# Scores kept with a row to a partition: norms from ScalarE's squares, rows scaled, then transposed by block transfers and VectorE

## The chip, the cores and the metric

The kernel runs on one core of one Trainium2 chip. The metric is device time in microseconds (us) for one execution. "Before" is the median of six executions. Five engines work on it: TensorE (PE in the profile, with PEld for its weight loads), VectorE (DVE), ScalarE (ACT), GpSimd (POOL), and SyncE (SP), which issues most DMAs.

## The reference

A graph network of two layers works on `x`, 64 batches of 256 nodes with 512 features, with one adjacency matrix of 256 x 256 zeros and ones. Cut to what is computed:

```
h   = relu(layernorm(x))
q, k, v = h @ Wq.T, h @ Wk.T, h @ Wv.T
rel = adj.T * (q @ k.T)                      # per batch, 256 x 256
rel = rel / norm(rel, over the last axis)    # each row n divided by its own norm
x   = x + rel @ v                            # layer 0
h   = relu(layernorm(x))
x   = x + (adj @ h) @ weight + bias          # layer 1
```

The row norm is the matter here. It is a sum over m for every row n of `rel`, and `rel @ v` also sums over m.

## The kernel before

**Tiling.** Work goes in 32 pairs of batches (`NP` = 32, `NB` = 2 batches in each). A pair has 512 tokens, held as `TC` = 4 chunks of 128 partitions, numbered c = 2b + n. Everything is float32. Most products are done by `winograd` (L165): a product of 2 x 2 blocks in seven block products instead of eight, collected in three PSUM banks (a, c, a, c, a, b, a). After each product a `take` reads the bank. In `project_v`, `project_g` and `scores`, takes 0, 1, 2 and 6 are ScalarE copies and takes 3, 4, 5 are VectorE adds; in `mix` all seven are VectorE adds. A product that adds to a bank must wait until the take before has read it: product 3 (bank c) waits for take 1, product 4 (bank a) for take 2, product 6 (bank a) for take 4.

**Stages of a pair.** `project_v` (L323) makes v. `project_g` (L305) makes G = h Wq'Wk, so that the scores are G h'. `scores` (L336) makes the masked scores in `rel`. `attend` (L368) makes `rel @ v` and adds it to x. `ln1` (L394) is the second layer norm, `gather` (L423) multiplies by the adjacency, and `mix` (L446) by the weight; `mix` ends the pair, and GpSimd issues the store.

**Scores before.** `rel` has m on the partitions and n along the free axis. That is the form that `attend` needs as its stationary operand (L384), but the norm's sum then runs over partitions. So ScalarE squares (L358), GpSimd adds the two halves of m into `sqs` (L365), and `attend` begins with four float32 products of `sqs` by a column of ones into the bank `pn` (L374), each 128 x 128 by one column and each recorded as two passes. ScalarE takes the root (L376), VectorE the reciprocal (L377), and the result scales the rows when `attend` adds to x (L387).

**Transposing h by blocks.** The layer norm of h for a later pair is written by ScalarE, then `place_blocks` (L282) moves its 32 x 32 blocks to their transposed places with 16 DMAs of 64 KB on SP's queue, and `transpose_blocks` (L292) turns the blocks in place with eight VectorE transposes of 128 x 256 (L298). There is one buffer `blocks`, so a `place_blocks` waits until the transposes of the one before have read it.

**Order of the work.** The setup and `pairs` (L507), up to the call of `steady`, are ordered by a planner. `steady` (L529) is written out by hand for PE, DVE and ACT: each of these runs its instructions in program order, and the `side` lists say after which product a step of another stage is put on its engine. SP and GpSimd are still ordered by the planner, and an instruction of `pairs` that the planner reckons ready late is put in among those of `steady`. In the loop, iteration i runs on PE: `attend(i)`, `project_v(i+1)`, `scores(i+1)`, `gather(i)`, `project_g(i+2)`, `mix(i)`. `transpose_blocks(i+3)` is done beside `gather(i)` and `place_blocks(i+4)` after `mix(i)`. The ends differ: the first pairs are prepared in `pairs`, with `scores(0)` and `project_g(1)` before the loop, and iteration 30 (`last_but_one`) has no `project_g`: it runs `gather(30)`, then at once `attend(31)`, then `mix(30)`.

Of the kernel before, what the change touches and what calls it, by code (L numbers as in the profile page):

```python
# [9 lines left out]
F32 = mybir.dt.float32  # L10
F32R = mybir.dt.float32r
I32 = mybir.dt.int32
# [7 lines left out]
def kernel(  # L20
# [55 lines left out]
    work = ctx.enter_context(tc.tile_pool(name="work", bufs=1))  # L76
    whole = ctx.enter_context(tc.tile_pool(name="whole", bufs=2))
    small = ctx.enter_context(tc.tile_pool(name="small", bufs=3))
    ps_m = ctx.enter_context(tc.tile_pool(name="ps_m", bufs=7, space=bass.MemoryType.PSUM))
    ps_n = ctx.enter_context(tc.tile_pool(name="ps_n", bufs=1, space=bass.MemoryType.PSUM))  # L80

    X, H, HL, G, GS, V, R, H2, Y = ({} for _ in range(9))

# [125 lines left out]
    def product_of_tokens(left, right):  # L209

        def product(bank, n, start):
            for b in range(NB):
                for d in range(HC):
                    nc.tensor.matmul(  # L214
                        bank[:, ts(b, P)], left[n][:, d, ts(b, P)], right[n][:, d, ts(b, P)],
                        start=(start and b == 0 and d == 0), stop=(d == HC - 1),
                        skip_group_check=True,
                    )
        return product
# [116 lines left out]
    def scores(i):  # L336

        left, right = HL.pop(i), G.pop(i)
        rel = work.tile([P, NB, NC, N], F32, tag="rel", name=f"rel_{i}")
        sq = work.tile([P, NB, NC, N], F32, tag="sq", name=f"sq_{i}")  # L340
        sqs = work.tile([P, NB, N], F32, tag="sqs", name=f"sqs_{i}")
        R[i] = (rel, sqs)

        def take(t, k, bank, first):
            dst = rel[:, :, t, ts(k, P)]
            src = bank[:, :HT_].rearrange("p (b n) -> p b n", b=NB)
            if first:
                nc.scalar.copy(dst, src)
            else:
                nc.vector.tensor_add(dst, src, dst)  # L350

        def mask(t):
            nc.vector.tensor_mul(
                rel[:, :, t], rel[:, :, t], adj_sb[:, t : t + 1, :].to_broadcast([P, NB, N])
            )

        def square(t):
            nc.scalar.activation(sq[:, :, t], rel[:, :, t], AF.Square)  # L358

        winograd(product_of_tokens(left, right), take, {5: [lambda: mask(0)]})  # L360
        return (
            lambda: mask(1),
            lambda: square(0),
            lambda: square(1),
            lambda: nc.gpsimd.tensor_tensor(sqs, sq[:, :, 0], sq[:, :, 1], ALU.add),  # L365
        )

    def attend(i, side={}):  # L368
        (rel, sqs), v, xt = R.pop(i), flat(V.pop(i)), flat(X[i])
        pn = ps_n.tile([P, TC], F32, tag="pn", name="pn")  # L370
        for b in range(NB):
            for n in range(NC):
                c = b * NC + n
                nc.tensor.matmul(pn[:, c : c + 1], sqs[:, b, ts(n, P)], ones, start=True, stop=True)  # L374
        rn = small.tile([P, TC], F32, tag="rn", name="rn")
        nc.scalar.activation(rn, pn, AF.Sqrt)  # L376
        nc.vector.reciprocal(rn, rn)  # L377
        for b in range(NB):
            for n in range(NC):
                c = b * NC + n  # L380
                pm = ps_m.tile([P, 512], F32, tag="pm", name="pu")
                for m in range(NC):
                    nc.tensor.matmul(  # L383
                        pm[:, :D], rel[:, b, m, ts(n, P)], v[:, b * NC + m, :],  # L384
                        start=(m == 0), stop=(m == NC - 1),
                    )
                nc.vector.scalar_tensor_tensor(  # L387
                    xt[:, c, :], pm[:, :D], rn[:, c : c + 1], xt[:, c, :],
                    op0=ALU.mult, op1=ALU.add,
                )  # L390
                run(side.get(c, ()))


# [64 lines left out]
                nc.sync.dma_start(out=outs[i][:, :, t], in_=xt[:, :, t])  # L458


    low = work.tile([P, NC * N], I32, tag="sqs", name="low")
# [5 lines left out]
    pf = ps_n.tile([P, TC], F32, tag="pn", name="pf")  # L467
# [39 lines left out]
    def pairs(exact):  # L507
        for j in range(1, 5):
            load(j)
        transposes_by_matmul(0)  # L510
        ln0_at_once(1)
        place_blocks(1)
        project_v(0)
        project_g(0)
        run(GS.pop(0))
        turned, sums = transpose_blocks(1)
        run(turned + sums)
        ln0_at_once(2)
        place_blocks(2)
        run(scores(0))  # L520
        project_g(1)
        turned, sums = transpose_blocks(2)
        run(turned + sums)
        ln0_at_once(3)
        place_blocks(3)
        with tc.manual_schedule(engines={EngineType.PE, EngineType.DVE, EngineType.Activation}):
            steady(exact)

    def steady(exact):  # L529


        for i in range(NP):
            last_but_one = i + 2 == NP
            if 0 < i < NP - 4:
                load(i + 4)
            if i + 1 < NP:
                stats, root, end, relus, uppers, lowers = ln1(i, exact)
                gs = GS.pop(i + 1)
                attend(i, {c: [stats[c]] for c in range(TC)})
                project_v(i + 1, {  # L540
                    0: [root, gs[0], end, relus[0], relus[1]],
                    1: [uppers[0], uppers[1], gs[1], lowers[0]],
                    2: [relus[2], lowers[1]],
                    3: [relus[3], uppers[2], uppers[3], gs[2]],
                    4: [lowers[2]],
                    5: [lowers[3], gs[3]],
                })
                mask, square0, square1, square_sum = scores(i + 1)
            turned, sums = [], []
            if i + 3 < NP:  # L550
                turned, sums = transpose_blocks(i + 3)
            if i + 1 < NP:
                y_steps = gather(i, exact, {
                    0: [mask, square0] + turned[0:2],
                    1: [square1, square_sum] + turned[2:4],
                    2: turned[4:6],
                    3: turned[6:8],
                })
            else:
                y_steps = gather(i, exact)  # L560
            if i + 2 < NP:
                project_g(i + 2, {
                    0: y_steps[0:1],
                    1: y_steps[1:3],
                    2: y_steps[3:4] + sums[0:1],
                    3: sums[1:2],
                    4: sums[2:3],
                    5: sums[3:4],
                })
            else:  # L570
                run(y_steps)
            if i + 4 < NP:
                stats, root, end, relus = ln0(i + 4)
                mix(i, {n: [stats[n]] for n in range(TC)} | {4: [root], 5: [end] + relus})
                place_blocks(i + 4)
            elif last_but_one:
                stats, root, end, relus, uppers, lowers = ln1(i + 1, exact)
                attend(i + 1, {c: [stats[c]] for c in range(TC)})
                mix(i, {
                    0: [root, end, relus[0], relus[1]],  # L580
                    1: [uppers[0], uppers[1], lowers[0]],
                    2: [relus[2], lowers[1]],
                    3: [relus[3], uppers[2], uppers[3], lowers[2]],
                    4: [lowers[3]],
                })
            else:
                mix(i)

    first = X[0], H[0]
    with tc.If(inexact < 1) as either:  # L590
# [32 lines left out]
```

## Time and profile before

| What | Value |
| --- | --- |
| median of six runs | 1797.51 us (1795.28 to 1798.89) |
| the profiled execution | 1797.57 us, span 1795.8 us |
| PE busy | 1765.1 us, 98% of the span |
| DVE busy | 1201.1 us, 67% |
| ACT busy | 571.1 us, 32% |
| POOL busy | 241.7 us, 13% |
| granted PE clock, mean | 0.995 |
| DMA packets under 512 B | 263120 of 290246 |
| one pair in the loop | 54.26 us from one `attend` to the next (852.84 to 907.10) |

In a line of the chain of waits the columns are start, duration, engine, tile and source line. A line of the timeline gives start, duration, engine, source line, operation, output and inputs with shapes, the number of instructions joined, and in brackets the idle time before it with what ended it. A line of windows gives, for a stretch, its length, the busy time and count of PE, PEld, DVE, ACT and POOL, and then the granted PE clock (1.00 is full), the DMA engines' busy share and GB/s.

### The profile page before, as it was taken

The page shows a single profiled execution, that of the slowest core. Times are in us where ns is not written, and L with a number is a line of the kernel's source. Part 1 is how long each engine was busy: PE and PEld are TensorE (multiplying, and loading weights), DVE is VectorE, ACT ScalarE, POOL GpSimd, SP SyncE. Part 2 cuts the span into 40 slices and gives each one's busy share as a digit, 9 for nine tenths or more (in the row PEclk, how much of TensorE's full clock was granted, in tenths as well). Part 3 has the DMA queues.
Part 4 walks back from the last instruction along what each step waited for, and adds up shares of the span by engine and source line. Part 5 has one row for each costly group of instructions (what it writes and reads, how often), then busy time and mean ns, then how long its engine had stood idle before and what let it go on. Part 6 is the DMA issues. An engine that isn't in the chain of part 4 may idle for free.

```text
span 1795.8 us, 22994 instructions
## 1 busy us (share of the span) xinstructions
PE 1765.1 (98%) x9030; PEld 1480.0 (82%) x9030; DVE 1201.1 (67%) x2216; ACT 571.1 (32%) x1071; POOL 241.7 (13%) x200
## 2 busy tenths in 40 slices
PE   7899999999999999999999999999999999999998
PEld 4778888888888888889888889888888888888886
DVE  5477666767666766766676766676767676666555
ACT  3233222333223333323332323332323332233321
POOL 0011111111101111101111101111111111011111
PEclk9999999999999999999999999999999999999999
DMA  6313321233311332311223211333212232111001
GB/s 222 47 24 71 70 45 46 52 71 71 71 40 35 68 71 71 71 36 36 71 71 70 55 47 41 71 71 71 48 50 45 71 71 71 42 45 32 24 24 49
DMA packets 290246, 105.93 MB, mean 59 GB/s; under 512 B 263120, under 2 KB 263120, under 8 KB 290128
## 3 DMA queue, kind: packets, MB, share of 16 engines
q1 hardware_dynamic: 279904, 68.19, 18.6%
q0 software_dynamic: 8592, 33.03, 5.0%
q10 hardware_dynamic: 1632, 3.15, 0.5%
q8 instruction: 72, 1.18, 0.3%
q14 instruction: 46, 0.38, 0.1%
HBM read 38.27 MB, written 33.55 MB: 40 GB/s over the span
## 4 chain that ended last, share of the span: by engine, by line
PE 93%; issue 4%; DVE 1%; DMA 0%; ACT 0%; POOL 0%; POOLq 0%; DVEq 0%
PE bank_a L202 24%; PE pu L383 12%; PE bank_a L190 12%; PE bank_c L202 12%; PE py L435 7%; PE bank_a L214 6%; PE bank_c L190 6%; PE bank_b L202 6%; PE bank_c L214 3%; PE bank_b L190 3%; PE bank_b L214 1%; PE pn L374 1%; DMA adj_sb<-in_adj_dram 0%; DVE h L416 0%; ACT h2c L245 0%
## 5 line engine op out<-in xcount | busy, mean ns | idle before, releaser
L383 PE MATMUL pu<-v,rel 128*128 128x512 f32 x512 | 227.5, 597 | 0.0
L408 POOL TENSOR_TENSOR x_ring<-x_ring,bias_bc 128x512 f32<-128x512 f32 x128 | 174.9, 1385 | 371.1 <-ACT h2c L245 371.1
L233 DVE BATCH_NORM_STATS2 st<-x_ring 128x6 f32<-128x512 f32 x256 | 175.8, 688 | 11.9 <-DMA x_ring<-in_x_dram 7.5
L383 PEld LDWEIGHTS pu<-v,rel 128*128 128x128 f32 x512 | 94.9, 190 | 107.2 <-issue 106.7
L416 DVE TENSOR_TENSOR h<-h2c,h 128x512 fp32r<-128x512 f32 x128 | 122.6, 976 | 63.1 <-ACT h L412 63.1
L451 DVE TENSOR_TENSOR x_ring<-bank_a,x_ring 128x512 f32<-128x512 f32 x128 | 88.5, 691 | 109.4 <-PE bank_a L202 105.6
L330 ACT COPY v<-bank_a 128x512 f32<-128x512 f32 x96 | 56.0, 584 | 321.0 <-PE bank_a L202 321.0
L313 ACT COPY g<-bank_a 128x512 f32<-128x512 f32 x96 | 56.2, 585 | 274.6 <-PE bank_a L190 274.6
L435 PE MATMUL py<-adjt_r,h 128*128 128x256 f32 x1024 | 130.6, 285 | 0.0
L435 PEld LDWEIGHTS py<-adjt_r,h 128*128 128x128 f32 x1024 | 124.8, 192 | 0.1
L455 POOL DMA_DIRECT2D out_dram<-x_ring x31 | 23.9, 770 | 747.9 <-issue 574.8
L202 PE MATMUL bank_a<-w_t,ys 128*128 128x256 f32 x512 | 121.1, 379 | 0.0
L202 PE MATMUL bank_a<-wv_t,hs 128*128 128x256 f32 x512 | 121.0, 379 | 0.0
L190 PE MATMUL bank_a<-hs,m_t 128*128 128x256 f32 x512 | 120.9, 379 | 0.0
L202 PEld LDWEIGHTS bank_a<-w_t,ys 128*128 128x128 f32 x512 | 97.1, 190 | 13.7 <-DVE x_ring L451 0.6
L202 PEld LDWEIGHTS bank_a<-wv_t,hs 128*128 128x128 f32 x512 | 97.3, 190 | 13.2
L190 PEld LDWEIGHTS bank_a<-hs,m_t 128*128 128x128 f32 x512 | 97.3, 190 | 13.2
L245 ACT ACTIVATE h2c<-x_ring,nb,rs 128x512 f32<-128x512 f32 x128 | 97.3, 806 | 30.0 <-DVE h L416 15.8
L245 ACT ACTIVATE h<-x_ring,nb,rs 128x512 f32<-128x512 f32 x124 | 90.8, 802 | 50.0 <-DVE nb L242 49.6
L387 DVE SCALAR_TENSOR_TENSOR x_ring<-pu,rn,x_ring 128x512 f32<-128x512 f32 x128 | 96.1, 751 | 11.6 <-PE pu L383 5.6
L238 ACT ACTIVATE rs<-rs 128x4 f32<-128x4 f32 x64 | 13.2, 207 | 266.2 <-DVE rs L237 266.2
L365 POOL TENSOR_TENSOR sqs<-sq 128x512 f32<-128x512 f32 x32 | 40.8, 1274 | 413.3 <-DVE ht L298 220.4
(124 smaller groups left out, 3263.0 us busy)
## 6 DMA issues: line engine op xcount, KB each, us to landing
x_ring<-in_x_dram SPq DMA_DIRECT2D x32, 1024.0 KB, 5.8
blocks<-h SPq DMA_DIRECT2D x496, 64.0 KB, 2.3
out_dram<-x_ring POOLq DMA_DIRECT2D x31, 1024.0 KB, 4.8
wk_sb<-in_L_gnn_Wk_dram ACTq DMA_DIRECT2D x4, 256.0 KB, 5.3
wq_sb<-in_L_gnn_Wq_dram SPq DMA_DIRECT2D x4, 256.0 KB, 6.4
wv_sb<-in_L_gnn_Wv_dram ACTq DMA_DIRECT2D x1, 1024.0 KB, 11.9
w_sb<-in_L_gnn_weight_dram ACTq DMA_DIRECT2D x1, 1024.0 KB, 16.0
out_dram<-x_ring SPq DMA_DIRECT2D x2, 512.0 KB, 4.2
```

The lines of the kernel that those rows point to most:

```text
L190: nc.tensor.matmul(bank[:, e * HT_ : (e + 1) * HT_], right[n][:, d, ts(e, P)], left[n][:, d, :], start=(start and e == 0 and d == 0), stop ...
L202: nc.tensor.matmul(bank[:, b * HD : (b + 1) * HD], left[n][:, d, ts(b, P)], right[n][:, d, :], start=(start and b == 0 and d == 0), stop=( ...
L214: nc.tensor.matmul(bank[:, ts(b, P)], left[n][:, d, ts(b, P)], right[n][:, d, ts(b, P)], start=(start and b == 0 and d == 0), stop=(d == H ...
L233: nc.vector.bn_stats(st[:, c, :], src[:, c, :])
L245: nc.scalar.activation(dst, src[:, c, :], AF.Relu, bias=nb[:, c : c + 1], scale=rs[:, c : c + 1])
L313: nc.scalar.copy(dst, src)
L383: nc.tensor.matmul(pm[:, :D], rel[:, b, m, ts(n, P)], v[:, b * NC + m, :], start=(m == 0), stop=(m == NC - 1),)
L387: nc.vector.scalar_tensor_tensor(xt[:, c, :], pm[:, :D], rn[:, c : c + 1], xt[:, c, :], op0=ALU.mult, op1=ALU.add,)
L408: nc.gpsimd.tensor_tensor(xt[:, c, :], xt[:, c, :], bias_bc, ALU.add)
L416: nc.vector.tensor_sub(dst[:, 1, c, :], whole_h[c], dst[:, 0, c, :].bitcast(F32))
L435: nc.tensor.matmul(pm[:, d, :], left[:, b * NC + m, ts(d0 + d, P)], right, start=(n == 0), stop=(n == len(terms) - 1),)
L451: nc.vector.tensor_add(dst, bank.rearrange("p (b e) -> p b e", b=NB), dst)
```

## The change

The two operands of the scores' products are exchanged, so that `rel` has n on the partitions: a row to a partition. The mask is now the transposed adjacency, and both halves of it are applied after the last product. The norm becomes four ScalarE squares of 128 x 256 that also sum along the row (`accum_out`), a root, a reciprocal, and four ScalarE copies that scale each row in place. Then `place` moves the 32 x 32 blocks with 16 DMAs of 32 KB on SP's queue into `placed`, and four VectorE transposes (`turn`) write `turned`, which `attend` uses. The squares by GpSimd's add, the products with ones, and the PSUM bank `pn` are gone (`ps_m` has 8 banks instead of 7), and `attend`'s last step is a plain add. In the loop, the scales and `place` come after take 0 of `project_g`, and the four turns after take 5 of `mix`.

```diff
-    ps_m = ... bufs=7
-    ps_n = ... bufs=1
+    ps_m = ... bufs=8
...
-                        bank[:, ts(b, P)], left[n][:, d, ts(b, P)], right[n][:, d, ts(b, P)],
+                        bank[:, ts(b, P)], right[n][:, d, ts(b, P)], left[n][:, d, ts(b, P)],
...
         def take(t, k, bank, first):
-            dst = rel[:, :, t, ts(k, P)]
+            dst = rel[:, :, k, ts(t, P)]
...
+        def square_sum(b, k):
+            nc.scalar.activation(square, rel[:, b, k], AF.Square, accum_out=rn[:, b, k : k + 1])
+        def root():
+            nc.scalar.activation(rn, rn, AF.Sqrt)
+        def inverse():
+            nc.vector.reciprocal(rn, rn)
+        def scale(b, k):
+            nc.scalar.activation(rel[:, b, k], rel[:, b, k], AF.Copy, scale=rn[:, b, k : k + 1])
+        def place():
+            rv = rel.rearrange("p b k (t m) -> p (b k t) m", m=P)
+            pv = placed.rearrange("p b k t n -> p (b k t) n")
+            for j in range(P // S):
+                for k in range(P // S):
+                    nc.sync.dma_start(out=pv[ts(j, S), :, ts(k, S)], in_=rv[ts(k, S), :, ts(j, S)])
+        def turn(b, k):
+            nc.vector.transpose(turned[:, b, :, k], placed[:, b, k])
+        def each(f):
+            return [(lambda b=b, k=k: f(b, k)) for k in range(NC) for b in range(NB)]
-        winograd(product_of_tokens(left, right), take, {5: [lambda: mask(0)]})
+        winograd(product_of_tokens(left, right), take)
...
     def attend(i, side={}):
-        pn = ps_n.tile([P, TC], F32, tag="pn", name="pn")
-        for b, n: nc.tensor.matmul(pn[:, c : c + 1], sqs[:, b, ts(n, P)], ones, start=True, stop=True)
-        nc.scalar.activation(rn, pn, AF.Sqrt)
-        nc.vector.reciprocal(rn, rn)
...
-                        pm[:, :D], rel[:, b, m, ts(n, P)], v[:, b * NC + m, :],
+                        pm[:, :D], rel[:, b, m, n], v[:, b * NC + m, :],
...
-                nc.vector.scalar_tensor_tensor(xt[:, c, :], pm[:, :D], rn[:, c : c + 1], xt[:, c, :], ...)
+                nc.vector.tensor_add(xt[:, c, :], pm[:, :D], xt[:, c, :])
...
-        run(scores(0))
+        scores_at_once(0)
...
                 y_steps = gather(i, exact, {
-                    0: [mask, square0] + turned[0:2],
-                    1: [square1, square_sum] + turned[2:4],
-                    2: turned[4:6],
-                    3: turned[6:8],
+                    0: masks + turned[0:1],
+                    1: squares[0:2] + turned[1:3],
+                    2: squares[2:4] + turned[3:5],
+                    3: [norm_root, inverse] + turned[5:8],
                 })
...
                 project_g(i + 2, {
-                    0: y_steps[0:1],
+                    0: scales + [place] + y_steps[0:1],
...
             else:
+                if last_but_one:
+                    run(scales + [place])
                 run(y_steps)
...
-                mix(i, {n: [stats[n]] for n in range(TC)} | {4: [root], 5: [end] + relus})
+                mix(i, {n: [stats[n]] for n in range(TC)} | {4: [root], 5: [end] + turns + relus})
...
             elif last_but_one:
+                run(turns)
                 attend(i + 1, {c: [stats[c]] for c in range(TC)})
...
             else:
-                mix(i)
+                mix(i, {5: turns} if i + 1 < NP else {})
```

More of the change, by code (lines that the diff above doesn't have):

```diff
@@ L78 @@
     small = ctx.enter_context(tc.tile_pool(name="small", bufs=3))
-    ps_m = ctx.enter_context(tc.tile_pool(name="ps_m", bufs=7, space=bass.MemoryType.PSUM))
-    ps_n = ctx.enter_context(tc.tile_pool(name="ps_n", bufs=1, space=bass.MemoryType.PSUM))
+    ps_m = ctx.enter_context(tc.tile_pool(name="ps_m", bufs=8, space=bass.MemoryType.PSUM))
     X, H, HL, G, GS, V, R, H2, Y = ({} for _ in range(9))
@@ L339, in scores @@
         rel = work.tile([P, NB, NC, N], F32, tag="rel", name=f"rel_{i}")
-        sq = work.tile([P, NB, NC, N], F32, tag="sq", name=f"sq_{i}")
-        sqs = work.tile([P, NB, N], F32, tag="sqs", name=f"sqs_{i}")
-        R[i] = (rel, sqs)
+        placed = work.tile([P, NB, NC, NC, P], F32, tag="placed", name=f"placed_{i}")
+        turned = work.tile([P, NB, NC, NC, P], F32, tag="turned", name=f"turned_{i}")
+        square = work.tile([P, N], F32, tag="square", name=f"square_{i}")
+        rn = small.tile([P, NB, NC], F32, tag="rn", name="rn")
+        R[i] = turned
         def take(t, k, bank, first):
-            dst = rel[:, :, t, ts(k, P)]
-            src = bank[:, :HT_].rearrange("p (b n) -> p b n", b=NB)
+            dst = rel[:, :, k, ts(t, P)]
+            src = bank[:, :HT_].rearrange("p (b m) -> p b m", b=NB)
             if first:
@@ L350, in take, with mask @@
                 nc.vector.tensor_add(dst, src, dst)
-        def mask(t):
+        def mask(k):
             nc.vector.tensor_mul(
-                rel[:, :, t], rel[:, :, t], adj_sb[:, t : t + 1, :].to_broadcast([P, NB, N])
+                rel[:, :, k], rel[:, :, k], adjt_sb[:, k : k + 1, :].to_broadcast([P, NB, N])
             )
-        def square(t):
-            nc.scalar.activation(sq[:, :, t], rel[:, :, t], AF.Square)
-        winograd(product_of_tokens(left, right), take, {5: [lambda: mask(0)]})
+        def square_sum(b, k):
+            nc.scalar.activation(square, rel[:, b, k], AF.Square, accum_out=rn[:, b, k : k + 1])
@@ L361, in scores @@
+        def turn(b, k):
[3 more added lines that the diff above has]
+        winograd(product_of_tokens(left, right), take)
         return (
[L362 to L365, printed above, removed]
-        )
+            [lambda: mask(0), lambda: mask(1)], each(square_sum), root, inverse, each(scale), place,
+            each(turn),
+        )
@@ L368, in attend, with scores_at_once @@
+    def scores_at_once(i):
+        masks, squares, root, inverse, scales, place, turns = scores(i)
+        run(masks + squares + [root, inverse] + scales + [place] + turns)
     def attend(i, side={}):
-        (rel, sqs), v, xt = R.pop(i), flat(V.pop(i)), flat(X[i])
-        pn = ps_n.tile([P, TC], F32, tag="pn", name="pn")
[L371 to L374, printed above, removed]
@@ L375, in attend @@
-        rn = small.tile([P, TC], F32, tag="rn", name="rn")
-        nc.scalar.activation(rn, pn, AF.Sqrt)
-        nc.vector.reciprocal(rn, rn)
+        rel, v, xt = R.pop(i), flat(V.pop(i)), flat(X[i])
         for b in range(NB):
@@ L383, in attend @@
                     nc.tensor.matmul(
-                        pm[:, :D], rel[:, b, m, ts(n, P)], v[:, b * NC + m, :],
+                        pm[:, :D], rel[:, b, m, n], v[:, b * NC + m, :],
                         start=(m == 0), stop=(m == NC - 1),
                     )
[L387 to L390, printed above, removed]
+                nc.vector.tensor_add(xt[:, c, :], pm[:, :D], xt[:, c, :])
                 run(side.get(c, ()))
@@ L458, in mix @@
                 nc.sync.dma_start(out=outs[i][:, :, t], in_=xt[:, :, t])
-    low = work.tile([P, NC * N], I32, tag="sqs", name="low")
+    low = work.tile([P, NC * N], I32, tag="h", name="low")
     nc.vector.tensor_single_scalar(
@@ L466 @@
     nc.vector.tensor_reduce(low_max, low, axis=mybir.AxisListType.X, op=ALU.max)
-    pf = ps_n.tile([P, TC], F32, tag="pn", name="pf")
+    pf = ps_m.tile([P, 512], F32, tag="pm", name="pf")
     nc.tensor.matmul(pf[0:1, 0:1], low_max, ones, start=True, stop=True)
@@ L547, in steady @@
                 })
-                mask, square0, square1, square_sum = scores(i + 1)
+                masks, squares, norm_root, inverse, scales, place, turns = scores(i + 1)
             turned, sums = [], []
```

## The prediction, made before the changed kernel was run

> **What bounds the kernel now.** I read the page first: which engine is full, and what the chain that ended last is made of.
>
> ```profile
> PE 1765.1 (98%) x9030; PEld 1480.0 (82%) x9030; DVE 1201.1 (67%) x2216; ACT 571.1 (32%) x1071; POOL 241.7 (13%) x200
> PE 93%; issue 4%; DVE 1%; DMA 0%; ACT 0%; POOL 0%; POOLq 0%; DVEq 0%
> blocks<-h SPq DMA_DIRECT2D x496, 64.0 KB, 2.3
> ```
>
> TensorE is the bound; work on other engines costs time only where TensorE comes to wait for it. The third line (DMA issues) prices a block transfer: 64 KB, 2.3 us to landing. Next, the chain in order of time at one pair's border:
>
> ```profile
> 904.59 1.73 PE bank_a L202 x8
> 906.32 0.79 PE pn L374 x8
> 907.10 6.97 PE pu L383 x16
> ```
>
> The norm's products hold TensorE for 0.79 us between `mix` and `rel @ v`. Third, the timeline there, for who would be late if they went:
>
> ```profile
> 904.63 0.69 DVE L451 TENSOR_TENSOR x_ring<-bank_b,x_ring 128x512 f32<-128x512 f32 x1 [0.96 <-PE bank_b L202]
> 905.43 0.16 DVE L242 SCALAR_TENSOR_TENSOR nb<-mv,rs 128x4 f32<-128x4 f32 x1
> 905.94 1.08 PEld L374 LDWEIGHTS pn<-ones,sqs 128*128 128x128 f32 x8
> 908.59 12.26 SPq L288 DMA_DIRECT2D blocks<-h  x16
> ```
>
> The four turns come after the second line, and the first load of `attend` can start where the third does. Last, both ends, where pairs don't overlap:
>
> ```profile
> 72.26 2.73 DVE L298 STREAM_TRANSPOSE ht<-blocks 128x256 f32<-128x256 f32 x8 [0.20 <-issue]
> 103.41 2.71 DVE L298 STREAM_TRANSPOSE ht<-blocks 128x256 f32<-128x256 f32 x8
> 107.35 3.78 PE L202 MATMUL bank_a<-wv_t,ht 128*128 128x256 f32 x8 [3.06 <-DVE v L332]
> 1746.34 4.07 PE L435 MATMUL py<-adjt_r,h 128*128 128x256 f32 x32
> 1752.07 7.11 PE L383 MATMUL pu<-v,rel 128*128 128x512 f32 x16
> ```
>
> and the granted clock after TensorE's wait of 3.06 us:
>
> ```profile
> 107.35:110.00 2.65, 2.65 (x6) 2.19 (x7) 2.65 (x5) 0.00 (x0) 0.00 (x0) 0.50 0.74 96
> 113.60:116.00 2.40, 2.40 (x24) 2.40 (x23) 0.01 (x1) 0.74 (x2) 0.00 (x0) 1.00 0.77 105
> ```
>
> After that wait the clock stays at half to about 113.5, over 6.2 us of work. A longer wait thus costs another 3.1 us.
>
> **In the loop: the gain.** Thirty pairs (1 to 30) have the 0.79 us in the open; those of pairs 0 and 31 lie in waits at the ends. The add in `attend` becomes plain: 751 ns (L387) to 691 (L451, also bank to x). The last one heads the chain of statistics and relus that makes TensorE wait 0.15 us in `project_v` (12.24 us for seven products of 1.727), so 0.06 comes off.
>
> **In the loop: the turns.** Each is an L298: 408 ns, starting 0.34 apart. The first group of `attend` needs the first turn only, the second group the third. That holds if waits follow the slices and not the whole tile, and they do: at 878.35 ScalarE writes a slice of `rel` while the first mask (877.91 to 878.60) works on slices interleaved with it. VectorE is free at 905.59. The transposes at 72.26 came 0.20 us behind a short reciprocal, so: start 905.79, end 906.20, load 906.25, 0.31 after 905.94. Loads run about 0.13 ahead (a load 0.27 late in `project_v` cost 0.14), leaving 0.18 us; without that gap, none. I take 0.18. The turns put the last take of `mix` at 907.2, before the first bank of `attend` is full (908.7): no cost.
>
> **In the loop: ScalarE.** Both masks now wait for take 6 (ends 878.72) and end by 880.1 instead of 879.44. A 128x512 square is 639 ns; a copy falls from 584 to 372 with half the columns, so a 128x256 square is 0.43, or 0.33 behind another. What the row sum adds no row shows: nothing to 0.2. Four squares between the copies of `gather` end it at 883.2 to 884.0, about where take 0 starts (883.91). The scales follow at 884.4: 0.33 plus 0.09 for an operand read per partition (a relu with two is 806 against 612 for a cast) is 0.42 each, to 886.1. Take 1 then ends at 886.7; product 3 loads at 886.95. No cost, with 0.4 us to spare.
>
> VectorE waits for the root, to 884.3 at worst, then ends three transposes (885.4), `y_steps` and one sum (4.2 us together before, the first at 1350 ns beside GpSimd's add that is now gone) by 889.0; take 3 came at 889.16. No cost. GpSimd's 1274 ns go at no gain.
>
> `place` starts at 886.1 on SP, idle since 867.6 and next needed at 908.6. Sixteen issues: 64 KB ones are 0.68 (10.86/16, first set) to 0.77 (12.26/16) apart, a large load holds SP 0.50; I take 0.62. With 2.1 to 2.3 to landing that is 9.3 + 2.1 = 11.4 us: landed at 897.5, eight before the turns. The cover is `project_g` and most of `mix`. Per pair: -0.79 - 0.06 + 0.18 = -0.67 us; times 30, **-20.1** (bounds: -25.5 with no wait for a turn, -16 with 0.32).
>
> **The end.** Iteration 30 has no `project_g`, so nothing covers squares, scales, place and turns. From the copies (1747.57 on), as above: squares, root and reciprocal end at 1751.7, scales at 1753.4, or 1753.8 with half of the possible row sum cost. Plus 11.4 and a turn with its signals (0.5): `attend(31)` starts at 1765.7 against 1752.07, 13.6 later, and the half clock adds 3.1: **+16.7** (14.5 to 20).
>
> **The start.** Before, the planner put the transposes of block set 1 behind the norm of pair 0 (72.26, though the set's DMAs were over by 60), and those of set 2 at 103.41, into `project_v(1)`, though the DMAs were idle from 88. So it reckons some 25 us for sixteen block transfers. New: masks end 68.3, inverse 69.7, transposes of set 1, `project_g(1)` from 70.3 to 85.5 at half clock first (before: to 86.66). Scales end 71.4, place lands 82.9, turns after take 5 at 84.4: `attend(0)` waits little. But set 2 is now queued on SP behind `place` and its transposes move, by the planner's reckoning of 13 us more, to the end of `scores(1)`, about 110. The interruption at 103 to 113 (3.06 of idle and 3.1 of clock) is gone, but set 3 may be placed only then: 112.8 + 11.5 + 2.3 = 126.6. Its transposes stand by hand in `gather(0)`, ahead of the inverse: scales to 130.4, take 1 to 131.1, while product 3 of `project_g(2)` was ready at 119.9. TensorE waits 11 us and loses 3.1; that stage ends at 141.1 against 134.5: **+6.6**. Bounds: -1.2 if set 2 keeps its place; +8.7 if SP takes set 2 before `place`, and `attend(0)` waits 13 us.
>
> **Sum.** The profiled execution took 1797.57 us (span 1795.8), the median 1797.51, so no shift: 1797.57 - 20.1 + 6.6 + 16.7 = 1800.8.
>
> **Two rules.** The Trainium skill, DMA: Bandwidth & Descriptors (Rules for kernel authors), speaks against `place`: below 64 KB a transfer is mostly overhead; Anatomy of one DMA gives 2.0 us fixed for each (on GpSimd's path). Sixteen in a row would be 33 us by it (estimate), and the sum about 1822. The trace's sixteen start 0.77 apart, so the fixed parts overlap. TensorE: Matmul & The Clock Gate (Part 1) gives a warm-up of about 3.4 us, not the 6.2 seen; by it each long wait costs 1.7 (estimate), and the sum is 1798.
>
> **Rivals.**
> - *ScalarE becomes the bound inside the pair* (slower). Take 1 queues behind four scales, and product 3 waits. It decides once scales start more than 0.52 us apart; at 0.62 it is 0.4 us in 30 pairs: +12, 1813 (1807 to 1822). For it: no row has this form. Against: the relu rows. 0.20.
> - *The ends cost less* (faster). The start stays hidden (-1.2), SP issues 32 KB at 0.50 apart (+14.5), the turns cost nothing in the loop (-25.5): 1785; halfway to the forecast, 1793. For it: smaller transfers, the planner's order unseen. 0.20.
> - *It doesn't do what it says*: waits go by whole tiles, so TensorE waits for all four turns, 1.0 us more per pair: 1831. Against: 878.35. Or the functions no longer share a table: a load is 1283 ns, but before had two in all with the same functions. 0.05.
>
> **Numbers.** The forecast has 0.55, its own range 1794 to 1807: the ends take back what the loop gains. About 0.2% (3.6 us) is what a measurement can tell from no change. Of the 0.55, 0.28 lies within it, 0.25 above, 0.02 below; the rivals add 0.20 and 0.05 above, and 0.18 below and 0.02 within. Faster 0.20, same 0.30, slower 0.50. The range 1789 to 1813 leaves out some 2 in 10.
>
> **What would show it.** Right: one pair 53.6 us; no line L374; a gap ahead of `pu` of 0.2; 15 us of idle TensorE after the last `gather` but one, and about 11 in the first `project_g` of the loop, each followed by half clock. Wrong: scales over 0.5 us apart and TensorE released by ScalarE in each `project_g`; the turns later than take 5; block set 3 landed before 119.

## The result: 0.3% slower, and the profile after

The changed kernel takes 1802.72 us (median of 16 runs, 1801.09 to 1804.35) against 1797.52 us for the one before (36 runs). The ratio is 1.0029 with an interval of 1.0022 to 1.0035. The profiled execution took 1803.25 us with a span of 1801.4 us, 5.6 us more than the span before.

First the page of the changed kernel: busy time by engine, the chain by engine, and the two block transfers among the DMA issues (count, size, median us to landing).

```profile
PE 1745.2 (97%) x8774; PEld 1448.6 (80%) x8774; DVE 1212.3 (67%) x2344; ACT 644.8 (36%) x1391; POOL 200.8 (11%) x168
PE 94%; SPq 1%; DMA 1%; ACT 1%; DVE 1%; issue 0%; ACTq 0%; DVEq 0%
blocks<-h SPq DMA_DIRECT2D x496, 64.0 KB, 2.3
placed<-rel SPq DMA_DIRECT2D x512, 32.0 KB, 2.0
```

TensorE has 19.9 us less to do in a span that is 5.6 us longer. SP's queue has appeared in the chain and the DMA's share of it has gone from 0% to 1%: TensorE now waits somewhere for a transfer. The chain of the changed kernel at a border of two pairs (start, duration, what) shows the gain and the first loss:

```profile
902.11 1.73 PE bank_b L201 x8
903.84 1.74 PE bank_a L201 x8
905.58 0.07 issue
905.65 7.11 PE pu L400 x16
```

The 0.79 us of `pn` are gone, but `pu` holds 7.11 us instead of 6.97, with 0.07 ahead of it. The timeline there says why:

```profile
903.88 0.69 DVE L465 TENSOR_TENSOR x_ring<-bank_b,x_ring 128x512 f32<-128x512 f32 x1 [0.96 <-PE bank_b L201]
904.69 0.16 DVE L241 SCALAR_TENSOR_TENSOR nb<-mv,rs 128x4 f32<-128x4 f32 x1
905.06 1.43 DVE L378 STREAM_TRANSPOSE turned<-placed 128x256 f32<-128x256 f32 x4 [0.21 <-issue]
905.62 0.30 PEld L400 LDWEIGHTS pu<-v,turned 128*128 128x128 f32 x2 [0.46 <-PE bank_a L201]
```

The first turn starts 0.21 us after the last step of the layer norm, and the first load of `attend` stands 0.11 us behind that turn's end (905.06 and at most 0.45 for one turn), not behind all four (906.49). The bracket names `bank_a`, but the time follows the turn: the first product (905.65) starts 0.59 after the first turn, and it does so too at both ends, in the lines below, where the bracket names the turn.

The two ends, by the timeline of the changed kernel. At the start:

```profile
74.36 3.20 SPq L375 DMA_DIRECT2D placed<-rel  x5
77.68 10.69 SPq L287 DMA_DIRECT2D blocks<-h  x16
88.41 7.16 SPq L375 DMA_DIRECT2D placed<-rel  x11
95.68 11.05 SPq L287 DMA_DIRECT2D blocks<-h  x16
90.09 2.73 DVE L297 STREAM_TRANSPOSE ht<-blocks 128x256 f32<-128x256 f32 x8 [2.96 <-DMA blocks<-h]
97.70 9.25 PE L400 MATMUL pu<-v,turned 128*128 128x512 f32 x16 [9.56 <-DVE turned L378]
```

SP takes five issues of pair 0's `place`, then all sixteen of block set 2, then the other eleven, and then block set 3 (from 95.68); `attend(0)` waits 9.56 us for `place`. At the end, in iteration 30:

```profile
1743.47 10.40 SPq L375 DMA_DIRECT2D placed<-rel  x16
1755.25 1.49 DVE L378 STREAM_TRANSPOSE turned<-placed 128x256 f32<-128x256 f32 x4 [10.79 <-DMA placed<-rel]
1755.84 9.62 PE L400 MATMUL pu<-v,turned 128*128 128x512 f32 x16 [16.00 <-DVE turned L378]
```

Sixteen issues 0.65 apart and the landing of the last of them stand in the open, and `attend` takes 9.62 and 9.25 us where a pair of the loop takes 7.1. The windows of the changed kernel show the granted clock, which stands behind the busy times and counts of the five engines, at 0.50 after both waits:

```profile
97.70:102.00 4.30, 4.30 (x5) 1.80 (x6) 1.34 (x4) 0.00 (x0) 0.00 (x0) 0.50 0.69 103
102.00:107.00 5.00, 5.00 (x13) 2.28 (x12) 4.20 (x10) 0.00 (x0) 0.00 (x0) 1.00 0.63 91
1755.80:1760.00 4.20, 4.16 (x5) 1.86 (x6) 1.30 (x4) 0.00 (x0) 0.00 (x0) 0.50 0.03 6
```

The ledger of the two profiled executions, from where `attend` and the stages start in the two chains:

| Stretch | before | after | difference |
| --- | --- | --- | --- |
| start to the end of `project_g(2)` | 134.48 | 141.38 | +6.9 |
| from there to `attend(30)` | 1586.62 | 1569.26 | -17.4 |
| `attend(30)` to `attend(31)` | 31.11 | 45.20 | +14.1 |
| `attend(31)` to the end of the span | 43.6 | 45.56 | +2.0 |

Together +5.6 us. In the loop a pair takes 53.70 us instead of 54.27.

### The profile page after: what moved, and what is told of

The parts are those of the page before. It is cut to its first block, busy times and chain, and to the rows that moved or that the text cites. A ratio compares the mean times of both kernels' runs of the same rounds, so it can differ in the third digit from the quotient of the medians.

```text
span 1801.4 us, 23762 instructions
## 1 busy us (share of the span) xinstructions
PE 1745.2 (97%) x8774; PEld 1448.6 (80%) x8774; DVE 1212.3 (67%) x2344; ACT 644.8 (36%) x1391; POOL 200.8 (11%) x168
## 4 chain that ended last, share of the span: by engine, by line
PE 94%; SPq 1%; DMA 1%; ACT 1%; DVE 1%; issue 0%; ACTq 0%; DVEq 0%
PE bank_a L201 24%; PE pu L400 13%; PE bank_c L201 12%; PE bank_a L189 12%; PE py L449 7%; PE bank_a L213 6%; PE bank_b L201 6%; PE bank_c L189 6%; PE bank_c L213 3%; PE bank_b L189 3%; PE bank_b L213 2%; DMA w_sb<-in_L_gnn_weight_dram 1%; SPq L375 1%; SPq L287 1%; DMA wk_sb<-in_L_gnn_Wk_dram 0%
## 5 line engine op out<-in xcount | busy, mean ns | idle before, releaser
L400 PE MATMUL pu<-v,turned 128*128 128x512 f32 x512 | 231.9, 606 | 28.4 <-DVE turned L378 26.0
L400 PEld LDWEIGHTS pu<-v,turned 128*128 128x128 f32 x512 | 96.5, 193 | 149.5 <-issue 136.2
L404 DVE TENSOR_TENSOR x_ring<-pu,x_ring 128x512 f32<-128x512 f32 x128 | 88.5, 691 | 32.8 <-PE pu L400 25.2
L297 DVE STREAM_TRANSPOSE ht<-blocks 128x256 f32<-128x256 f32 x248 | 86.9, 408 | 3.2 <-DMA blocks<-h 3.0
```

The costliest lines, as they stand in the source:

```text
L297: nc.vector.transpose(ht[:, d, half].rearrange("p (b n) -> p b n", b=NB), by_half[:, :, half, d])
L400: nc.tensor.matmul(pm[:, :D], rel[:, b, m, n], v[:, b * NC + m, :], start=(m == 0), stop=(m == NC - 1),)
L404: nc.vector.tensor_add(xt[:, c, :], pm[:, :D], xt[:, c, :])
```

## The experiments

Theory: the loop gains what the products held, less a wait for the first turn; the start and the end each lose a wait for `place`, the start's because of the order of issues on SP, the end's because nothing covers it, and each brings the half clock. The rivals: ScalarE's scales or VectorE cost time inside the pair; transfers or landing, not order and issue, bound the two ends. Times below are medians, ratios are to the kernel before.

**Pair 31 turned by TensorE** (`e1_end_by_tensore`). Eight TensorE transposes and two copies take the place of `place` and the turns, for that pair alone.

```diff
+        def by_tensore(b):
+            pt = ps_m.tile([P, 512], F32, tag="pm", name="pr")
+            for t, k: nc.tensor.transpose(pt[:, ts(t * NC + k, P)], rel[:, b, k, ts(t, P)], ident)
+            (nc.vector.tensor_copy if b else nc.scalar.copy)(turned[:, b], pt)
...
-                    run(scales + [place])
+                    run(scales + by_tensore of both batches)
...
-                run(turns)
```

> The changed kernel, with one part undone: for pair 31 alone the scaled rows are transposed by eight TensorE transposes into two PSUM banks and copied back (one copy on ScalarE, one on VectorE), instead of 16 block transfers and four turns. Theory (the end costs 16.1 us, because nothing covers the transfers): the start of the last rel @ v falls from 1755.8 to about 1746, since the wait is then squares, scales, transposes and copies (some 6 us after the last gather product); half clock may still follow, as the wait stays over 3 us. About 1792.5 us, the loop's pairs unchanged at 53.70. Rival (the loss is spread over the loop, and the end only shows it): the time falls by less than 4 us, 1799 or more.

Measured: 1789.67 us, 0.9955 (0.9941 to 0.9968), 13.0 us below the changed kernel. `attend(30)` to `attend(31)` falls from 45.20 to 33.66 us, where the kernel before has 31.11: all but 2.6 of the 14.1 us by which this stretch had grown are `place` with its turns. In all it is some 3 us more than I expected, and more than twice the 5.2 us by which the changed kernel is slower. The timeline of this run:

```profile
1741.70 0.33 PE L384 MATMUL pr<-ident,rel 128*128 128x128 f32 x1 [2.46 <-ACT rel L368]
1743.72 8.65 PE L412 MATMUL pu<-v,turned 128*128 128x512 f32 x16 [0.24 <-ACT turned L389]
```

The half clock still follows, behind a wait of 2.46 us: `attend(31)` takes 8.65.

**Pair 0 turned by TensorE** (`e2_start_by_tensore`).

```diff
-        run(masks + squares + [root, inverse] + scales + [place] + turns)
+        run(masks + squares + [root, inverse] + scales + by_tensore of both batches)
```

> The changed kernel, with one part undone: for pair 0 alone the scaled rows are transposed by TensorE as in the other run, so that nothing of pair 0 stands on the DMA queue between block sets 1 and 2. Theory (the start costs 4.6 us beside the setup, as attend(0) waits 9.6 us for turns whose transfers were split by block set 2): that wait goes, set 2's transposes may fall into project_v(1) again as before, which cost 6.2 us there; together about 1798 us. Rival (the 6.9 us are the setup's, a matter of chance): no change, 1802 to 1803.

Measured: 1796.43 us, 0.9992 (0.9983 to 1.0001), 6.3 us below the changed kernel. The timeline of this run at the start:

```profile
76.11 40.62 SPq L287 DMA_DIRECT2D blocks<-h  x32
86.69 7.03 PE L412 MATMUL pu<-v,turned 128*128 128x512 f32 x16
107.20 3.51 PE L201 MATMUL bank_a<-wv_t,ht 128*128 128x256 f32 x8 [3.09 <-DVE v L331]
```

Block sets 2 and 3 go out on SP with nothing of `place` among them, `attend(0)` starts at 86.69 without a wait, and the old interruption of `project_v(1)` is back. So the start swaps a wait of 9.6 us for one of 3.1.

**The turns after take 4 of `mix` instead of take 5** (`e3_turns_after_take4`).

```diff
-                mix(i, {...} | {4: [root], 5: [end] + turns + relus})
+                mix(i, {...} | {4: [root] + turns, 5: [end] + relus})
...
-                mix(i, {5: turns} if i + 1 < NP else {})
+                mix(i, {4: turns} if i + 1 < NP else {})
```

> The changed kernel, with one size of its schedule changed: the four turns stand after take 4 of mix (behind the small step ahead of the root) instead of after take 5. Theory (in each of 28 pairs the first load of rel @ v waits 0.28 us for the first turn, the transfers having landed some 6 us before): the wait goes, a pair takes 53.4 instead of 53.70, and the time falls by 7.8 us to about 1795. Rival (the turns only move the delay, to take 5 and the end of the relus, and TensorE waits elsewhere in mix or for the transfers): 1802 or more.

Measured: 1793.55 us, 0.9979 (0.9970 to 0.9989), 9.2 us below the changed kernel. The timeline of this run at a border:

```profile
895.88 1.42 DVE L378 STREAM_TRANSPOSE turned<-placed 128x256 f32<-128x256 f32 x4
897.99 0.16 DVE L241 SCALAR_TENSOR_TENSOR nb<-mv,rs 128x4 f32<-128x4 f32 x1
898.25 0.41 PEld L400 LDWEIGHTS pu<-v,turned 128*128 128x128 f32 x2
```

The turns are done one product earlier, the first load has no wait in brackets, and the pair takes 53.37 us instead of 53.70. The wait for the first turn cost 0.33 us in each of 28 pairs (in the last two of the loop no norm step stands ahead of the turns, and they take 53.60 and 53.37 already in the changed kernel).

**The kernel before, with the norm's products made twice** (`e4_before_norm_twice`).

```diff
-        for b in range(NB):
+        for b in range(2 * NB):
+            b = b % NB
             for n in range(NC):
...
                 nc.tensor.matmul(pn[:, c : c + 1], sqs[:, b, ts(n, P)], ones, start=True, stop=True)
```

> The kernel before, with the products of the norm by the column of ones issued twice (the second time over the same results). Theory (each set holds TensorE for 0.79 us with nothing beside it): 30 pairs by 0.79 and about 1 us at each end, 1797.5 + 25 = 1822.5 us, a pair 55.05. Rival (they run partly in the shadow of something else, so that taking them away could only have gained the 0.57 us a pair that was seen): 17 us, about 1815.

Measured: 1826.45 us, 1.0161 (1.0148 to 1.0175); the pair goes from 54.27 to 55.17, +0.90 for the second set. I had expected the 0.79 of the chain's line.

**The kernel before without the norm's products** (`e11_before_without_norm`).

```diff
-                nc.tensor.matmul(pn[:, c : c + 1], sqs[:, b, ts(n, P)], ones, start=True, stop=True)
...
-        nc.scalar.activation(rn, pn, AF.Sqrt)
-        nc.vector.reciprocal(rn, rn)
+        nc.vector.memset(rn, 1.0)
```

> The kernel before without the norm's products, root and reciprocal (the rows are multiplied by 1, so the result lacks the norm). It gives the most that the removal can bring in the loop. Theory: the 0.79 us of the products lie wholly in the open, the pair goes from 54.27 to 53.48, the ends keep their times, and thirty pairs make 1797.5 - 23.7 = 1773.8. The rival, that part of it is taken back as soon as the products go (the first load of attend waits for the last takes, or the statistics are late): pair 53.6 to 54.0 and 1778 to 1790.

Measured: 1764.40 us, 0.9818 (0.9804 to 0.9831), below both theories. Its chain at a border:

```profile
888.11 1.73 PE bank_a L202 x8
889.84 6.87 PE pu L381 x16
```

Without `pn` the piece of `pu` is 6.87 us long, where it is 6.97 behind `pn`. So the products are worth 0.79 + 0.10 = 0.89, and the pair falls from 54.27 to 53.37, -0.90. Thirty pairs make 27 us; the other 6 of the 33 (4.7 of the 31.7 between the two profiled spans) lie at the ends (`attend(0)` starts 2.7 us earlier, at 84.36), where I had put the products, with TensorE's wait for their operand, at nothing. This kernel keeps the dearer add (0.75 us, L385) and reaches the same 53.37 as the one with early turns and the plain add: the plain add is worth nothing in the loop.

**Two more ScalarE copies behind the scales** (`e10_two_more_copies`).

```diff
-                    0: scales + [place] + y_steps[0:1],
+                    0: scales + [place] + (two copies of rel[:, b, 0] into square) + y_steps[0:1],
```

> In the loop ScalarE makes two more copies of 128 x 256, of no use, right behind place, so that take 1 of project_g comes some 0.75 to 0.84 us later (0.33 to 0.42 each). In the profile of the changed kernel take 1 ends at 885.81 and product 3 starts at 886.41, with its first load some 0.13 ahead, so ScalarE has 0.46 to spare. Theory (the cover is that thin and no thinner): TensorE waits about 0.3 to 0.4 us in each of 30 project_g, the pair goes from 53.70 to 54.0 to 54.1, the time to 1812 to 1815. If the scales cost something already: the pair grows by the whole 0.75 to 0.84, and the time is 1825 or more. If the cover is much wider than it looks: 1802.7.

Measured: 1811.29 us, 1.0079 (1.0066 to 1.0093); the pair takes 54.00 us, +0.30. In its timeline:

```profile
887.66 0.83 ACT L387 COPY square<-rel 128x256 f32<-128x256 f32 x2
888.40 0.58 ACT L312 COPY g<-bank_c 128x512 f32<-128x512 f32 x1
889.03 1.59 PEld L189 LDWEIGHTS bank_c<-hs,m_sb 128*128 128x128 f32 x8 [0.44 <-ACT g L312]
```

Product 3's first load now waits for ScalarE's take 1, as the rival of the prediction had it. The added work of 0.74 us (887.66 to 888.40) cost 0.30, so 0.44 us were to spare.

**Rows scaled in the add, no scales** (`e8_rows_scaled_in_add`).

```diff
-        run(masks + squares + [root, inverse] + scales + [place] + turns)
+        run(masks + [place] + squares + [root, inverse] + turns)
...
-                    0: masks + turned[0:1],
+                    0: masks + [place] + turned[0:1],
...
-                    0: scales + [place] + y_steps[0:1],
+                    0: y_steps[0:1],
...
-                    run(scales + [place])
+                    pass
...
-                nc.vector.tensor_add(xt[:, c, :], pm[:, :D], xt[:, c, :])
+                nc.vector.scalar_tensor_tensor(xt[:, c, :], pm[:, :D], rn[:, b, n : n + 1], xt[:, c, :], ...)
```

> The changed kernel without ScalarE's scales: rows go unscaled through place, which is issued right after the masks, and attend's add multiplies by the reciprocal as before the change. Theory: in the loop the scales cost nothing now, so the pair keeps its 53.70 and gains back only the 0.06 us of the dearer last add (53.76); at the end place(31) starts some 6.6 us earlier (after the masks instead of after the scales), at the start place(0) goes out before block set 2 and attend(0) waits little, but set 2 then interrupts project_v(1): 1802.7 - 6.6 - 6 + 1.8 = 1792. The rival, that the scales cost time in the loop: the pair falls below 53.6 and the time below 1788.

Measured: 1792.82 us, 0.9976 (0.9966 to 0.9985), 9.9 us below the changed kernel. The pair keeps its 53.70: the scales cost nothing there, and neither does the dearer add. All of the gain is at the ends (`attend(30)` to `attend(31)` 39.55). The time is as I expected, but at the start not for the reason I gave, as the timeline of SP in this run shows:

```profile
67.87 3.86 SPq L375 DMA_DIRECT2D placed<-rel  x6
73.44 10.71 SPq L287 DMA_DIRECT2D blocks<-h  x16
84.19 6.52 SPq L375 DMA_DIRECT2D placed<-rel  x10
```

`place` starts 6.5 us earlier than in the changed kernel (2.1 of it because this profile's setup was faster, see the last section), and still only six of its issues go ahead of block set 2. SP even sits idle from 71.73 to 73.44, with ten issues ready behind set 2: it goes by a fixed order and does not take what is ready. `attend(0)` still waits 7.17 us.

**Pair 0's `place` from GpSimd's queue** (`e6_place0_on_gpsimd`).

```diff
+            queue = nc.gpsimd if i == 0 else nc.sync
...
-                    nc.sync.dma_start(out=pv[...], in_=rv[...])
+                    queue.dma_start(out=pv[...], in_=rv[...])
```

> Only the place of pair 0 is issued from GpSimd's queue instead of SP's. Theory: the wait of 9.56 us before attend(0) is the order on SP, where the sixteen issues of block set 2 (10.7 us) stand between the fifth and the sixth of place. Then place(0) lands by about 87, attend(0) starts at 88 to 90 with at most 1 to 3 us of wait, and the time falls by 6 to 9 us, to 1794 to 1797, unless set 2 and its transposes then hold up project_v(1). The rival, that both sets share the DMA engines and would be as late in two queues: attend(0) still at 96 to 98 and 1802.7.

Measured: 1795.98 us, 0.9990 (0.9981 to 0.9999), 6.7 us below the changed kernel. Its timeline:

```profile
73.88 9.23 POOL L376 DMA_DIRECT2D placed<-rel  x16 [70.61 <-ACT rel L368]
85.96 1.41 DVE L379 STREAM_TRANSPOSE turned<-placed 128x256 f32<-128x256 f32 x4
86.87 7.03 PE L401 MATMUL pu<-v,turned 128*128 128x512 f32 x16
107.36 3.68 PE L201 MATMUL bank_a<-wv_t,ht 128*128 128x256 f32 x8 [3.08 <-DVE v L331]
```

The same sixteen transfers, now beside those of set 2 instead of among them, are in place by 85.96, and `attend(0)` waits for nothing, while the old interruption of `project_v(1)` is back. That settles the start's wait for `place`: it is the order on SP, not the transfers.

**Half of pair 31's `place` on ScalarE's queue** (`e7_end_place_two_queues`).

```diff
-                    nc.sync.dma_start(out=pv[...], in_=rv[...])
+                    (nc.scalar if i + 1 == NP and k % 2 else nc.sync).dma_start(out=pv[...], in_=rv[...])
```

> The sixteen issues of pair 31's place are halved between SP's queue and ScalarE's. If the issue (0.65 apart on one queue, 10.4 us for sixteen) bounds it and not the transfer, eight take 5.2 us, turns start some 5 us earlier and the time is 1797.5 to 1798. If the transfers bound it (the DMA engines, the landing), nothing changes: 1802.7. Only that pair's transfers are moved, so nothing else in the trace should differ.

Measured: 1796.17 us, 0.9993 (0.9984 to 1.0002), 6.5 us below the changed kernel. Its timeline at the end:

```profile
1742.10 5.17 SPq L375 DMA_DIRECT2D placed<-rel  x8
1742.11 5.51 ACTq L375 DMA_DIRECT2D placed<-rel  x8
1748.95 1.43 DVE L378 STREAM_TRANSPOSE turned<-placed 128x256 f32<-128x256 f32 x4 [5.86 <-DMA placed<-rel]
```

Two queues issue side by side at about the pace of one each (0.65 and 0.69 apart); `attend(30)` to `attend(31)` falls by 4.93 us to 40.27. So the issue on one queue, not the transfers, bounds how soon the last block lands. The profiled span fell by 7.1 us; its other parts are 0.8 in `attend(31)` (8.77 us, see the last section) and 1.4 at the start, which this edit does not touch.

**TensorE kept busy ahead of `attend(31)`** (`e5_end_kept_busy`).

```diff
+                for _ in range(17):
+                    nc.tensor.matmul(pw_, ident, w_sb[:, 0], start=True, stop=True)
                 run(turns)
```

> Seventeen products of 128 x 512 with no use for the result (some 14.8 us at 0.87 each) fill TensorE's wait of 16.0 us before attend(31). If the clock's drop in that wait is what makes attend(31) 9.62 us instead of 6.97, it is 6.97 again, TensorE waits about 1 us for the turns, and the whole is 2.65 us shorter: 1800.1. The rival, that attend(31) is slow because its later turns or its banks come late: it stays at 9.6 and the time at 1802.7.

Measured: 1800.47 us, 1.0015 (1.0006 to 1.0024), 2.25 us below the changed kernel. In its timeline the products without use (seventeen, each recorded as two passes) fill the wait, and in its windows the clock after it is 1.00:

```profile
1739.20 14.75 PE L596 MATMUL warm<-w_sb,ident 128*128 128x512 f32 x34
1755.35 7.10 PE L400 MATMUL pu<-v,turned 128*128 128x512 f32 x16 [1.40 <-DVE turned L378]
```
```profile
1755.30:1762.50 7.20, 7.15 (x17) 3.34 (x18) 5.66 (x13) 0.00 (x0) 0.00 (x0) 1.00 0.00 1
```

From `attend(31)` to the end it is 43.05 us instead of 45.56: the half clock costs 2.5 us, as a thing of its own beside the wait.

**The three edits together** (`e9_all_three`: pairs 0 and 31 by TensorE, turns after take 4).

> The three edits on one kernel: pairs 0 and 31 turned by TensorE transposes and ScalarE/VectorE copies instead of block transfers, the four turns of the other pairs after take 4 of mix. If the three costs (start, end, wait for the first turn) lie on separate stretches of the path, their gains add up: 1802.7 - 13.0 - 6.3 - 9.2 = 1774.2, some 1.3% faster than the kernel before. The rival, that they share a wait (a start that is late anyway catches up in the loop, or TensorE is held by something else once the turns are early): between 1780 and 1790.

Measured: 1776.29 us, 0.9881 (0.9866 to 0.9896). The pair is 53.37. The gains add up but for 2.1 us of 28.5; what became of those was not settled (four executions, which lie between 1774.36 and 1776.77).

**The same, with the rows scaled in the add** (`e12_all_and_scaled_in_add`: `place` or the TensorE transposes right behind the masks, no scales).

> The kernel with all three edits, and without ScalarE's scales: unscaled rows are placed or transposed right behind the masks, and attend's add multiplies by the reciprocal. Theory: the loop has no cost from either side of the scales, so the pair stays at 53.37; at the two ends TensorE's transposes no longer wait for squares, root and scales (they waited 4.3 us at the start and 2.5 at the end), of which the start gives back part, since project_g(1) then waits for the transposes of block set 1: 1776.3 - 2 - 2 = 1772. The rival, that both ends are held by other work by now: 1776. If the dearer add (0.75 us instead of 0.69) does cost time in the loop: pair 53.43 and 1774.

Measured: 1769.78 us, 0.9851 (0.9835 to 0.9868), the fastest here with a norm in it: 1.5% below the kernel before, 1.8% below the changed one. Its timeline at the end:

```profile
1722.17 1.04 PE L384 MATMUL pr<-ident,rel 128*128 128x128 f32 x8
1723.89 0.57 ACT L389 COPY turned<-pr 128x512 f32<-128x512 f32 x1
1724.51 7.13 PE L412 MATMUL pu<-v,turned 128*128 128x512 f32 x16 [1.30 <-ACT turned L389]
```

A wait of 16.0 us has become 1.30, and the granted clock is 1.00 throughout `attend(31)`.

## Why the prediction was right, and where its steps were off

The forecast was 1800.8 us in 1789 to 1813; 1802.72 was measured. The ends do take back what the loop gains. The signs that the prediction named came in the loop and at the end (53.70 a pair, no line of the norm's products, a gap ahead of `pu`, 16.0 us of idle TensorE and then half clock), but not at the start. By steps:

**The loop: -17.4 instead of -20.1.** Three of its terms were mis-sized, and partly cancel. The products were worth 0.90 a pair, not 0.79: their line in the chain leaves out the 0.10 by which they held up the first load of `pu`. The plain add, put at -0.06, was worth nothing (53.37 with either add, and 53.70 with either); the 0.15 us of idle in `project_v` were not shortened by it, since its last piece is 1.86 to 1.87 us in all these chains. The wait for the first turn, put at 0.18, was 0.33, at the bound that I gave without the slack that loads seemed to have, and in 28 pairs instead of 30. So -0.90 + 0.33 = -0.57 a pair instead of -0.67. That waits follow slices, not the whole tile, was right.

**ScalarE and VectorE: right.** In the timeline of the changed kernel the row sum has an instruction of its own:

```profile
879.99 0.42 ACT L359 ACTIVATE square<-rel 128x256 f32<-128x256 f32 x1
880.31 0.19 ACT L359 ACTIVATION_READ_ACCUMULATOR square<-rel 128x1 f32 x1
883.64 1.70 ACT L368 ACTIVATE rel<-rel,rn 128x256 f32<-128x256 f32 x4
885.25 0.56 ACT L312 COPY g<-bank_c 128x512 f32<-128x512 f32 x1
```

0.19 us each, at the upper end of "nothing to 0.2"; the scales are 0.42 apart as worked out. Take 1 ends at 885.81 ahead of product 3 at 886.41, and the 0.44 us to spare that the two copies found are the predicted 0.4. The rival in which ScalarE becomes the bound had the right place and, by the two copies, about the right price (what is added less 0.4); its condition (scales over 0.52 apart) was not met.

**`place` in the loop: right.** It issues from 885.37 for 10.40 us, 0.65 apart against the 0.62 that I took, and by the median of 2.0 us to landing it is in place some seven us ahead of the turns (905.06).

**The end: +16.1 instead of +16.7.** `attend(31)` comes 14.1 us later behind `attend(30)` instead of 13.6. The half clock made `attend(31)` 2.65 us longer instead of 3.1, and 2.0 of that remain at the end of the span. From the first issue at 1743.47 to the first turn at 1755.25 it is 11.8 us, and two queues issue side by side. By the 2.0 us fixed for each transfer in the Trainium skill, DMA: Bandwidth & Descriptors (Anatomy of one DMA, which is about GpSimd's path), sixteen in a row would be about 33 us (the prediction's estimate); here the fixed parts overlap. The half clock cost 1.6 to 2.65 us behind the waits for `place` (`e10` and the changed kernel), and 3.1 behind the interruption of `project_v(1)` in the kernel before. The warm-up of about 3.4 us in the Trainium skill, TensorE: Matmul & The Clock Gate (Part 1), would cost 1.7 (estimate): the measured costs begin near it and go to nearly twice as much.

**The start: the size near (+6.9 against +6.6), the mechanism wrong.** The step that failed is the planner's order. I had block set 2 queued behind `place` and its transposes moved to 110, so that `project_g(2)` would wait 11 us. Instead SP has set 2 in the middle of `place`, which is nearly the case that I kept as the upper bound (+8.7, `attend(0)` waits 13). Set 3 is issued from 95.68 and its last issue ends at 106.73, well before 119, which the prediction had named as a sign of being wrong, and `project_g(2)` waits for nothing. `attend(0)` starts 10.7 us later, of which 2.3 are from the setup, and pays 2.3 for the clock; the interruption of `project_v(1)` (3.06, and about 3.1 for the clock) is gone, since the transposes of set 2 at 90.09 lie in the wait. The 2.3 of the setup are not the change's: its second product came 0.6 us later, and TensorE lost its clock there in this execution and not in the one before, while four other kernels with the changed setup (`e2`, `e3`, `e8`, `e10`) have that product within 0.2 us of the kernel before and at full clock. So the start costs 4.6 us by the change itself. The chosen sum was near the result by chance; its bounds were sound.

## To carry to other kernels

A step that leaves the critical path in a loop is worth its line in the chain plus what it delays behind it (here 0.79 and 0.10), so the surest price is a run without it. A chain of transfers that the loop hid was in the open at the first and the last pass: price the ends apart, and do those passes by another engine if it is idle there, for the gain of the loop is small against one uncovered chain (16 us here against 0.57 a pair). Where two transfers share a queue, look up the order in which they are issued, since SP's queue did not take what was ready here, and where a wait appears, look whether the step is simply put one product too late.

## What the runs showed of the hardware

The same wait does not always lower TensorE's clock. In the setup every run has TensorE idle for 2.57 to 2.61 us ahead of the second product of `project_v(0)`. The timelines before (first line) and after (second):

```profile
36.08 1.97 PE L202 MATMUL bank_c<-wvt_sb,ht 128*128 128x256 f32 x8 [2.58 <-DVE ht L156]
```
```profile
36.67 3.27 PE L201 MATMUL bank_c<-wvt_sb,ht 128*128 128x256 f32 x8 [2.58 <-DVE ht L155]
```

That product takes 1.96 to 1.97 us in the profiles of before, `e2`, `e3`, `e7`, `e8` and `e10`, and 2.78 to 3.65 in those of after, `e1`, `e4`, `e5`, `e6`, `e9`, `e11` and `e12`: about the same idle time, and both groups hold the setup of before and that of after. Between 36.8 and 38.8 us the granted clock is 1.00 in the first group's experiments and 0.50 to 0.58 in the second's. It moves a single profile by some 1.7 us, which is as large as terms that were argued over here; how often it comes in the executions without a profile is not known. Nor does the half clock last a fixed time: after the same wait of 16.0 us `attend(31)` took 9.62, 9.52, 9.48, 9.19 and 8.55 us in five kernels.

A VectorE addition of 128 x 512 that took 1.37 us beside GpSimd's addition (`ys`, 882.01 before) takes 0.65 in the changed kernel, where that is gone. Neither number reached the time, since VectorE had room there.
